# Second attention pass of a quantized transformer block: the side work of the score loop cut into one piece per step, layer-norm groups shifted by two token tiles, the rounding issued behind the evacuations, and the last tiles in pairs

## The chip, the cores and the metric

One NeuronCore of a Trainium2 chip runs the whole program. The metric is the device time of one execution in microseconds (us); lower is better. The engines are TensorE (PE in the profile; its weight loads are PEld), VectorE (DVE), ScalarE (ACT), GpSimd (POOL) and SyncE (SP), which issues DMAs.

## The reference

Four transformer blocks L0 to L3 run one after the other on `x`, 4 sequences of 1024 tokens of 288 features (16 heads of 18). The change lies in block L2 ("Block 2"), a block whose attention is quantized with one scale for a whole tensor:

```python
def _fake_quant(x, n_bits, always_zero=False):
    levels = float(2 ** n_bits - 1)
    if always_zero:
        delta = max(x) / levels;  zp = 0
    else:
        delta = (max(x) - min(x)) / levels;  zp = round(-min(x) / delta)
    xq = clip(round(x / delta) + zp, 0.0, levels)
    return (xq - zp) * delta

def _quant_attention(x, ctx, Wq, Wk, Wv, Wo, bo):
    q, k, v = heads(x @ Wq), heads(ctx @ Wk), heads(ctx @ Wv)
    q, k, v = _fake_quant(q), _fake_quant(k), _fake_quant(v)
    probs = softmax(q k^T / sqrt(HD))
    probs = _fake_quant(probs, always_zero=True)
    return (probs @ v) @ Wo + bo

n1 = _ln(h);  h = h + _quant_attention(n1, n1, Wq1, Wk1, Wv1, Wo1, bo1)
n2 = _ln(h);  h = h + _quant_attention(n2, encoder_hidden_states, Wq2, Wk2, Wv2, Wo2, bo2)
n3 = _ln(h);  ... gated feed-forward ...
```

The self-attention's probabilities are rounded with a scale that needs the largest probability of all heads and rows. So the kernel goes over the scores twice: a first pass finds sums and maxima, the second one computes the scores again, rounds and multiplies by the values. The queries of the cross-attention, `n2 @ Wq2`, need their minimum and maximum over all tokens before they can be rounded.

## The kernel before

The tokens are 32 tiles of 128 (`NT = 32`, 8 to a sequence). `fq_passes` holds both passes. The second pass runs over 8 halves (4 sequences, 2 halves of 512 queries each); each half is one call of `attend_levels`: 4 groups of 4 heads, and in each group 8 steps, one for every 128 keys. So a half has 32 steps and the pass 256. A step does this:

- four matmuls (L3573) put the scores of 4 heads into two PSUM tiles of two banks each; there are three such tiles
- ScalarE takes the exponential of each (L3582, two instructions a step) into `e`, which has two buffers
- VectorE rounds `e` to bfloat16 levels `eb` (L3585; three buffers)
- the values matmuls (L3556) of the step two before are issued from the list `late`; after a group's eighth step VectorE copies the accumulator to `oT` (L3564)
- `aside()` takes one piece of side work from the list `side`, a list of Python generators; a piece ends at a `yield`.

The side work of a half is:

- `shifts`: for 4 tiles of the next half, GpSimd copies three terms into a padded tile (L2556), TensorE transposes it (L2562), and VectorE adds the result to the queries (L2563)
- `output(t0, oT)`: for the 4 tiles of the half before, the output projection (4 float32 matmuls a tile, L3234, each of two TensorE instructions), added to the residual `x` by VectorE (L3244)
- `queries(t0)`: the layer norm of those same 4 tiles, which have to be finished first: statistics (L1437, L1438), a chain of small VectorE instructions for 1/sqrt of the variance (L1442 to L1457), then per tile the norm `h` (VectorE L3256, GpSimd L3260 and L3261), the bias on `x` (GpSimd L1866), three transposes (L3268), their evacuation by VectorE (L3274), the query projection (3 float32 matmuls, L3282), its evacuation (VectorE L3289), a maximum and a minimum (L811, L812), and a store to DRAM (SP, L3291).

The first half has no `output` and no `queries`; those of the last half run after the loop, and then `fq_tail` begins, which needs the minimum and maximum over all of them. Small PSUM tiles (`ps1`) have two buffers, shared by the accumulator of the values, which holds one of them for a group's eight steps, and all side work.

The program is traced in this order, and the framework then orders each engine's instructions itself: an instruction that it takes to be ready may go ahead of an earlier one that it takes not to be. On the chip every engine works through its own list in order, with semaphores for the dependences.

Of the kernel before, what the change touches and what calls it, by code (L numbers as in the profile page):

```python
# [1179 lines left out]
class Fast(Net):  # L1180
# [250 lines left out]
    def norm_stats_slow(self, t0, m, eps):  # L1431
# [4 lines left out]
        for j in range(m):  # L1436
            nc.vector.bn_stats(st[:, j, :], self.x[:, t0 + j, :])  # L1437
            nc.vector.bn_aggr(mv[:, j, :], st[:, j, :])  # L1438
            if j % 4 == 3:
                yield  # L1440
        ve = self.stat([P, NTB], "ve")[:, :m]
# [6 lines left out]
        for k in range(3):  # L1448
            t = self.stat([P, NTB], "lnt")[:, :m]
            nc.vector.scalar_tensor_tensor(t, ve, -0.5, y, ALU.mult, ALU.mult)  # L1450
            nc.vector.tensor_tensor(t, t, y, ALU.mult)
            rstd = self.sm.tile([P, NTB], F32, tag=f"rstd{k}", name="rstd", bufs=8 if k == 2 else 4)
            rstd = rstd[:, :m]
            nc.vector.scalar_tensor_tensor(rstd, t, 1.5, y, ALU.add, ALU.mult)
            y = rstd
        nmr = self.sm.tile([P, NTB], F32, tag="nmr", name="nmr", bufs=8)[:, :m]
# [1536 lines left out]
    def fq_passes(self, w, q, step, raw, rawq, qmx, qmn, side, aside):  # L2993

        tc, nc = self.tc, self.nc
        with ExitStack() as es:
# [230 lines left out]
            def output(t0, oT):  # L3227

                yield
                yield  # L3230
                for j in range(4):
                    ps = self.ps1()
                    for k in range(NG):
                        nc.tensor.matmul(  # L3234
                            ps[:, :C],
                            lhsT=oT[:, k, j * P : (j + 1) * P],
                            rhs=wo[:, k, :],
                            start=(k == 0),
                            stop=(k == NG - 1),
                        )  # L3240
                        if k == 1:
                            yield
                    xt = self.x[:, t0 + j, :]
                    nc.vector.tensor_tensor(xt, xt, ps[:, :C], ALU.add)  # L3244
                    yield

            def queries(t0):

                rstd, nmr, _ = self.norm_stats_of(t0, 4, 1e-5)
                yield  # L3250
                hs, hTs = {}, {}
                for j in range(4 + 3):
                    if j < 4:
                        t = t0 + j
                        h = hs[j] = ot.tile([P, C], F32, tag="h2", name="h2", bufs=3)
                        nc.vector.tensor_scalar(  # L3256
# [5 lines left out]
                        self.add_bias(t, bo2)  # L3262
                        yield

                    if 0 <= j - 2 < 4:
                        ps = self.ps1()
                        for c in range(NC3):
                            nc.tensor.transpose(  # L3268
                                ps[:CK, c * P : (c + 1) * P],
                                hs[j - 2][:, c * CK : (c + 1) * CK],  # L3270
                                self.idf,
                            )
                        hT = hTs[j - 2] = ot.tile([CK, NC3, P], F32, tag="hT2", name="hT2")
                        nc.vector.tensor_copy(  # L3274
                            hT, ps[:CK, : NC3 * P].rearrange("p (c t) -> p c t", t=P)
                        )
                        yield
                    if 0 <= j - 3 < 4:
                        t = t0 + j - 3
                        ps = self.ps1()  # L3280
                        for c in range(NC3):
                            nc.tensor.matmul(  # L3282
                                ps[:, :C], lhsT=hTs[j - 3][:, c, :], rhs=wq2[:, c, :],
                                start=(c == 0), stop=(c == NC3 - 1),
                            )
                            if c == 0:
                                yield
                        y = ot.tile([P, C], F32, tag="y2", name="y2", bufs=1)
                        nc.vector.tensor_copy(y, ps[:, :C])  # L3289
                        self.min_max(qmx[:, t, :], qmn[:, t, :], y.unsqueeze(1))  # L3290
                        nc.sync.dma_start(rawq[t // NTB][:, t % NTB, :], y)  # L3291
                        yield
# [249 lines left out]
    def attend_levels(self, ep, qT, keys, v, b, qh, oT, step, late, aside):  # L3542
# [23 lines left out]
        for g in range(NG):  # L3566
            kz = keys(g)
            for kt in range(NTB):
# [14 lines left out]
                eb = ep.tile([P, 4, 512], BF16, tag="eb", name="eb", bufs=3)  # L3583

                nc.vector.tensor_scalar(eb, e, MAGIC, MAGIC, ALU.add, ALU.subtract)  # L3585
                late.append((values, g, kt, eb))
                if len(late) > 2:
                    st = late.pop(0)
                    st[0](*st[1:])
                aside()  # L3590

# [106 lines left out]
```

## Time and profile before

| | us |
|---|---|
| median of 3 runs | 4913.63 (4906.7 to 4917.26) |
| the profiled execution | 4914.71 |
| its span in the profile | 4913.0 |
| score loop of the second pass (first to last L3582) | 2347.7 to 2900.3 = 552.6 |
| its 8 halves, from the first L3582 of each | 61.1, 71.2, 69.4, 73.4, 69.6, 70.6, 69.5, 67.8 |
| after the loop, to the end of the last L812 | 2900.3 to 2939.1 = 38.8 |

The span is the time from the first to the last instruction of the program in the profile. The halves and their ends are read off the starts of the L3582 instructions in the trace. Busy times of overlapping instructions of one engine are counted once.

### The profile page before, as it was taken

Reading aid. Unit: us, or ns where it says so; the run is one execution under the profiler, and the core shown is the slowest. Engines: PE = TensorE matmul, PEld = TensorE weight load, DVE = VectorE, ACT = ScalarE, POOL = GpSimd, SP = SyncE. Lnnn points to the kernel's source line nnn. Section 1 sums busy time; section 2 is a strip of 40 time slices with the busy share of each in tenths; the row PEclk is TensorE's granted clock in tenths of the full one; section 3 lists DMA queues with packets and bytes.
Section 4 is the critical chain, followed back from the end, with each engine's and each line's share of the span. In section 5 each row is a group of like instructions: output and inputs, shape, how many; then the busy total and the mean of one; then the engine's idle time right before and its main releaser. Section 6 shows DMA issues by size and latency. Waiting matters only on the chain. (4 is left out here: it accounts for less than half of the span.)

```text
span 4913.0 us, 63515 instructions
## 1 busy us (share of the span) xinstructions
PE 4274.3 (87%) x23227; PEld 1733.7 (35%) x23227; DVE 3050.2 (62%) x6797; ACT 2986.3 (61%) x4219; POOL 1164.0 (24%) x1780
## 2 busy tenths in 40 slices
PE   4999998889988979998798873799998999998786
PEld 2223223445565411110233332445453223223444
DVE  8355445876644589999778878334244355445885
ACT  2776775666642279998888854122113776775664
POOL 2001001433212576420112225111111001002553
PEclk9999999889999955555688885799998999998898
DMA  3000002110001221000000022101000000001000
GB/s 85 3 5 22 12 8 72 41 35 16 3 13 56 105 68 33 26 6 0 22 25 25 23 85 57 50 13 34 1 3 15 4 4 22 14 7 40 17 17 18
DMA packets 137699, 135.97 MB, mean 28 GB/s; under 512 B 69276, under 2 KB 114972, under 8 KB 135712
## 3 DMA queue, kind: packets, MB, share of 16 engines
q1 hardware_dynamic: 136176, 128.13, 8.7%
q0 software_dynamic: 1200, 3.69, 0.3%
q8 instruction: 184, 3.01, 0.3%
q14 instruction: 139, 1.14, 0.1%
HBM read 79.92 MB, written 43.47 MB: 25 GB/s over the span
## 5 line engine op out<-in xcount | busy, mean ns | idle before, releaser
L2137 ACT ACTIVATE e<-ps 128x1024 f32<-128x1024 f32 x1024 | 993.7, 1022 | 411.8 <-PE ps L2127 403.9
L2127 PE MATMUL ps<-qT,kT 32*128 32x512 f32 x4096 | 624.6, 648 | 2.3 <-DVE sext L2049 2.3
L3164 DVE TENSOR_REDUCE top<-e 128x2 f32<-128x2048 f32 x256 | 563.6, 2298 | 14.8 <-ACT e L3157 14.6
L2083 PE MATMUL ps<-e,v 128*32 128x512 f32 x4096 | 556.4, 614 | 9.0 <-DVE oT L2094 9.0
L3533 PE MATMUL ps<-qk 32*128 32x512 bf16 x1024 | 499.9, 604 | 40.7 <-ACT e L3157 38.9
L3582 ACT ACTIVATE e<-ps 128x1024 f32<-128x1024 f32 x512 | 484.3, 1055 | 77.6 <-PE ps L3573 60.3
L3157 ACT ACTIVATE e<-ps 128x1024 f32<-128x1024 f32 x512 | 520.6, 1154 | 6.8 <-PE ps L3533 3.7
L1862 POOL TENSOR_TENSOR x<-x,y 128x288 f32<-128x288 f32 x192 | 152.5, 806 | 838.3 <-DVE y L1861 488.5
L3585 DVE TENSOR_SCALAR eb<-e 128x2048 bf16<-128x2048 f32 x256 | 320.5, 1256 | 46.5 <-ACT e L3582 44.1
L3573 PE MATMUL ps<-qk,kz 64*128 64x512 bf16 x1024 | 228.7, 444 | 42.7 <-ACT e L3582 39.3
L2600 PE MATMUL psf<-hT,w 128*128 128x512 f32 x576 | 257.9, 600 | 0.6 <-ACT hT L2592 0.6
L2127 PEld LDWEIGHTS ps<-qT,kT 32*128 32x128 f32 x4096 | 184.9, 185 | 201.3 <-issue 128.2
L2083 PEld LDWEIGHTS ps<-e,v 128*32 128x32 f32 x4096 | 81.3, 108 | 403.5 <-issue 344.3
L3533 PEld LDWEIGHTS <-qk 32*128 32x128 bf16 x1024 | 53.0, 100 | 465.2 <-issue 464.2
L3482 ACT ACTIVATE gl<-psf,bf 128x512 f32<-128x512 f32 x72 | 46.1, 685 | 269.9 <-PE psf L2604 265.5
L1477 POOL TENSOR_TENSOR h<-h,g 128x288 f32<-128x288 f32 x112 | 91.4, 817 | 443.8 <-ACT h L1474 434.2
L3486 DVE SCALAR_TENSOR_TENSOR u<-psf,bf,gl 128x512 f32<-128x512 f32 x72 | 51.2, 747 | 218.2 <-ACT gl L3482 218.2
L1979 POOL TENSOR_TENSOR v<-y,wv1b 128x288 f32<-128x288 f32 x64 | 51.5, 810 | 560.6 <-DVE y L1976 560.6
L278 PEld LDWEIGHTS <-qT 98*128 98x128 bf16 (+2 forms) x1344 | 132.1, 104 | 126.0 <-issue 37.4
L2094 DVE COPY oT<-ps 128x512 f32<-128x512 f32 x64 | 44.2, 690 | 212.1 <-PE ps L2083 212.1
L3157 ACT ACTIVATION_READ_ACCUMULATOR e<-ps 128x1 f32 x512 | 173.3, 338 | 0.0
L2600 PEld LDWEIGHTS psf<-hT,w 128*128 128x128 f32 x576 | 109.7, 192 | 132.9 <-issue 124.0
(526 smaller groups left out, 7825.3 us busy)
## 6 DMA issues: line engine op xcount, KB each, us to landing
raw<-y SPq DMA_DIRECT2D x32, 432.0 KB
in<-raw SPq DMA_DIRECT2D x30, 432.0 KB
kz<-qk SPq DMA_DIRECT2D x128, 64.0 KB
wn<-in_L_wfc SPq DMA_DIRECT2D x12, 432.0 KB
x<-in_x SPq DMA_DIRECT2D x4, 1152.0 KB
vvo<-vt SPq DMA_DIRECT2D x16, 288.0 KB
vo<-vvo SPq DMA_DIRECT2D x4, 1152.0 KB
rawq<-y SPq DMA_DIRECT2D x32, 144.0 KB
```

Source lines behind the costliest of these rows:

```text
L278: self.nc.tensor.matmul(out, lhsT=lhs[:, k, :], rhs=rhs[:, k, c0:c1], start=(k == 0), stop=(k == kc - 1))
L1862: nc.gpsimd.tensor_tensor(self.x[:, t, :], self.x[:, t, :], y, ALU.add)
L2083: nc.tensor.matmul(acc[i * HP : (i + 1) * HP, :], lhsT=st["v"][:, kt, h * (D + 1) : h * (D + 1) + HP], rhs=es_[i // 2][:, i % 2, :], start ...
L2127: nc.tensor.matmul(pss[i // 2][:, i % 2, :], lhsT=self.row_tile(kT, i)[:, kt * P : (kt + 1) * P], rhs=self.row_tile(qT, i)[:, qh * 512 : ( ...
L2137: nc.scalar.activation(e, ps, AF.Exp, scale=SCALE)
L2600: nc.tensor.matmul(o, lhsT=lhs(i)[:, c, :], rhs=rhs(i)[:, c, :], start=(c == 0), stop=False)
L3157: nc.scalar.activation(e[:, j, :].rearrange("p (a n) -> p a n", a=2), sc, AF.Exp, scale=rstep, accum_out=sums[:, t, h0 + j : h0 + j + 1],)
L3164: nc.vector.tensor_reduce(top[:, t, h0 : h0 + 2], e, AX.X, ALU.max)
L3533: self.last = self.nc.tensor.matmul(ps[:, c, :], lhsT=self.row_tile(qT, i)[:, g, qt * P : (qt + 1) * P], rhs=self.row_tile(kT, i)[:, g, c ...
L3573: nc.tensor.matmul(pss[i][:, n, :], lhsT=kz[rows, i, kt * P : (kt + 1) * P], rhs=qT[rows, g, qh * 512 : (qh + 1) * 512], start=True, stop= ...
L3582: nc.scalar.activation(e[:, 2 * n : 2 * n + 2, :], ps, AF.Exp, scale=step)
L3585: nc.vector.tensor_scalar(eb, e, MAGIC, MAGIC, ALU.add, ALU.subtract)
```

## The change

It touches the side work of the second pass, three lines of `attend_levels` and what runs after the loop.

1. One generator per half, `beside_half(n, oT)`, takes the place of `shifts`, `output` and `queries`. A piece is now one of: one tile's shift; one of the 4 matmuls of an output tile (the fourth with the residual add and the tile's statistics); one third of a query tile (transposes and their copy; two matmuls; the third matmul with the copy, maximum, minimum and store). For a middle half this makes 2 + 8 + 8 + 2 + 12 = 32 pieces.
2. The tiles are normalized in groups: {0,1}, {2..5}, ..., {22..25}, {26,27}, {28,29}, {30,31}. A group is complete after the second output tile of a half. Its chain (`norm_chain`, cut into four pieces) and its norms, one tile to a piece, are issued beside the third and fourth output tiles, and its queries follow in the last 12 pieces.
3. In the loop, the norm's scale and shift (L3256 before, on VectorE) is a GpSimd instruction.
4. The tile `hT2` has one buffer where it had two, `h2` has four where it had three.
5. In `attend_levels` the values matmuls of two steps before and the side piece are traced ahead of the rounding of the step.
6. The last half takes group {22..25} and {26,27}; its 36 pieces are 4 more than its steps. After the loop, tiles 28 to 31 go in two pairs: output of two, their norms on VectorE (`norm_dve`), output of two, queries of the first pair, norms of the second, queries of the second. There the evacuations are ScalarE copies.

```diff
--- before.py
+++ after.py
@@ -1438,6 +1438,16 @@
             nc.vector.bn_aggr(mv[:, j, :], st[:, j, :])
             if j % 4 == 3:
                 yield
+        at = self.norm_chain(mv, m, eps)
+        while True:
+            try:
+                next(at)
+            except StopIteration as end:
+                return end.value
+
+    def norm_chain(self, mv, m, eps):
+
+        nc = self.nc
         ve = self.stat([P, NTB], "ve")[:, :m]
         nc.vector.tensor_scalar(ve, mv[:, :, 1], eps, None, ALU.add)
 
@@ -1453,6 +1463,7 @@
             rstd = rstd[:, :m]
             nc.vector.scalar_tensor_tensor(rstd, t, 1.5, y, ALU.add, ALU.mult)
             y = rstd
+            yield
         nmr = self.sm.tile([P, NTB], F32, tag="nmr", name="nmr", bufs=8)[:, :m]
         nc.vector.scalar_tensor_tensor(nmr, mv[:, :, 0], -1.0, rstd, ALU.mult, ALU.mult)
         return rstd, nmr, mv[:, :, 0]
@@ -3224,80 +3235,129 @@
             bo2 = self.load_bc(at, w["bo2"], C, "bo2")
             wq2 = self.load_w(at, w["Wq2"], C, "wq2")
 
-            def output(t0, oT):
-
+            mvs, normed = {}, {}
+            groups = [range(0, 2)] + [range(t, t + 4) for t in range(2, NT - 6, 4)]
+            groups += [range(t, t + 2) for t in range(NT - 6, NT, 2)]
+            group_of = {t: n for n, ts in enumerate(groups) for t in ts}
+
+            def out_tile(t0, oT, j):
+
+                t = t0 + j
+                ps = self.ps1()
+                for k in range(NG):
+                    nc.tensor.matmul(
+                        ps[:, :C],
+                        lhsT=oT[:, k, j * P : (j + 1) * P],
+                        rhs=wo[:, k, :],
+                        start=(k == 0),
+                        stop=(k == NG - 1),
+                    )
+                    if k < NG - 1:
+                        yield
+                xt = self.x[:, t, :]
+                nc.vector.tensor_tensor(xt, xt, ps[:, :C], ALU.add)
+                n = group_of[t]
+                if n not in mvs:
+                    mvs[n] = self.sm.tile([P, NTB, 2], F32, tag="mvk", name="mvk", bufs=8)
+                st = self.sm.tile([P, NTB, 6], F32, tag="st", name="st", bufs=2)
+                nc.vector.bn_stats(st[:, 0, :], xt)
+                nc.vector.bn_aggr(mvs[n][:, t - groups[n][0], :], st[:, 0, :])
                 yield
+
+            def norms(n, dve):
+
+                m = len(groups[n])
+                chain = self.norm_chain(mvs.pop(n)[:, :m], m, 1e-5)
+                while True:
+                    try:
+                        next(chain)
+                    except StopIteration as end:
+                        stats = end.value
+                        break
+                    yield
                 yield
...
+                rstd, nmr, _ = stats
+                for j, t in enumerate(groups[n]):
+                    h = normed[t] = ot.tile([P, C], F32, tag="h2", name="h2", bufs=4)
+                    if dve:
+                        self.norm_dve(h, t, stats, j, g2, b2)
+                    else:
+                        nc.gpsimd.tensor_scalar(
                             h, self.x[:, t, :], rstd[:, j : j + 1], nmr[:, j : j + 1],
                             ALU.mult, ALU.add,
                         )
                         nc.gpsimd.tensor_tensor(h, h, g2, ALU.mult)
                         nc.gpsimd.tensor_tensor(h, h, b2, ALU.add)
-                        self.add_bias(t, bo2)
+                    self.add_bias(t, bo2)
+                    yield
+
+            def query(t, copy):
+
+                h = normed.pop(t)
+                ps = self.ps1()
+                for c in range(NC3):
+                    nc.tensor.transpose(
+                        ps[:CK, c * P : (c + 1) * P], h[:, c * CK : (c + 1) * CK], self.idf
+                    )
+                hT = ot.tile([CK, NC3, P], F32, tag="hT2", name="hT2", bufs=1)
+                copy(hT, ps[:CK, : NC3 * P].rearrange("p (c t) -> p c t", t=P))
+                yield
+                ps = self.ps1()
+                for c in range(NC3):
+                    nc.tensor.matmul(
+                        ps[:, :C], lhsT=hT[:, c, :], rhs=wq2[:, c, :],
+                        start=(c == 0), stop=(c == NC3 - 1),
+                    )
+                    if c == 1:
                         yield
...
+                y = ot.tile([P, C], F32, tag="y2", name="y2", bufs=1)
+                copy(y, ps[:, :C])
+                self.min_max(qmx[:, t, :], qmn[:, t, :], y.unsqueeze(1))
+                nc.sync.dma_start(rawq[t // NTB][:, t % NTB, :], y)
+                yield
+
+            def beside_half(n, oT):
+
+                turns = shifts(*divmod(n + 1, 2)) if n + 1 < 2 * B else iter(())
+                if n:
+                    for _ in range(2):
+                        next(turns, None)
                         yield
...
+                    t0 = 4 * (n - 1)
+                    for j in range(2):
+                        yield from out_tile(t0, oT, j)
+                    extra = norms(n - 1, False)
+                    for j in range(2, 4):
+                        for _ in out_tile(t0, oT, j):
+                            next(extra, None)
+                            yield
+                for _ in turns:
+                    if n:
+                        next(extra, None)
+                    yield
+                if n:
+                    for _ in extra:
+                        pass
+                    extra = norms(n, False) if n == 2 * B - 1 else iter(())
+                    for t in groups[n - 1]:
+                        for _ in query(t, nc.vector.tensor_copy):
+                            next(extra, None)
+                            yield
+                    for _ in extra:
+                        pass
+                    if n == 2 * B - 1:
+                        for t in groups[n]:
+                            yield from query(t, nc.vector.tensor_copy)
 
             late = []
+            oT = None
             for b in range(B):
                 for qh in range(2):
-                    side[:0] = [shifts(*divmod(2 * b + qh + 1, 2))] if 2 * b + qh + 1 < 2 * B else []
+                    n = 2 * b + qh
+                    side.append(beside_half(n, oT))
                     oT = ot.tile([P, NG, 512], F32, tag="oT", name="oT")
 
-                    def keys(g, turn=(2 * b + qh) * NG):
+                    def keys(g, turn=n * NG):
                         if turn + g + 1 < 2 * B * NG:
                             spread(turn + g + 1)
                         return kzs[(turn + g) % 2]
@@ -3305,12 +3365,22 @@
                     self.attend_levels(ep, qk[:, b, 0], keys, v, b, qh, oT, rstep, late, aside)
                     while side:
                         aside()
-                    t0 = b * NTB + qh * 4
-                    side += [output(t0, oT), queries(t0)]
             for st in late:
                 st[0](*st[1:])
-            while side:
-                aside()
+            for n in (2 * B, 2 * B + 1):
+                for t in groups[n]:
+                    for _ in out_tile(NT - 4, oT, t % 4):
+                        pass
+                if n == 2 * B:
+                    for _ in norms(n, True):
+                        pass
+            for n in (2 * B, 2 * B + 1):
+                for t in groups[n]:
+                    for _ in query(t, nc.scalar.copy):
+                        pass
+                if n == 2 * B:
+                    for _ in norms(n + 1, True):
+                        pass
 
     def fq_tail(self, w, kq, keep, rawq, mx, nmn, beside):
 
@@ -3580,14 +3650,13 @@
                 e = ep.tile([P, 4, 512], F32, tag="e", name="e")
                 for n, ps in enumerate(pss):
                     nc.scalar.activation(e[:, 2 * n : 2 * n + 2, :], ps, AF.Exp, scale=step)
-                eb = ep.tile([P, 4, 512], BF16, tag="eb", name="eb", bufs=3)
-
-                nc.vector.tensor_scalar(eb, e, MAGIC, MAGIC, ALU.add, ALU.subtract)
-                late.append((values, g, kt, eb))
-                if len(late) > 2:
+                if len(late) > 1:
                     st = late.pop(0)
                     st[0](*st[1:])
                 aside()
+                eb = ep.tile([P, 4, 512], BF16, tag="eb", name="eb", bufs=3)
+                nc.vector.tensor_scalar(eb, e, MAGIC, MAGIC, ALU.add, ALU.subtract)
+                late.append((values, g, kt, eb))
 
 
 @with_exitstack
```

More of the change, by code (lines that the diff above doesn't have):

```diff
@@ L3225, in fq_passes @@
             wq2 = self.load_w(at, w["Wq2"], C, "wq2")
-            def output(t0, oT):
-                yield
-                yield
[L3231 to L3256, printed above, removed]
+            mvs, normed = {}, {}
+            groups = [range(0, 2)] + [range(t, t + 4) for t in range(2, NT - 6, 4)]
@@ L3261, in queries @@
                         nc.gpsimd.tensor_tensor(h, h, b2, ALU.add)
-                        self.add_bias(t, bo2)
-                        yield
[L3265 to L3276, printed above, removed]
-                        yield
@@ L3278, in queries @@
[L3278 to L3292, printed above, removed]
+                    self.add_bias(t, bo2)
@@ L3582, in attend_levels @@
                     nc.scalar.activation(e[:, 2 * n : 2 * n + 2, :], ps, AF.Exp, scale=step)
+                if len(late) > 1:
+                    st = late.pop(0)
+                    st[0](*st[1:])
+                aside()
                 eb = ep.tile([P, 4, 512], BF16, tag="eb", name="eb", bufs=3)
@@ L3586, in attend_levels @@
                 late.append((values, g, kt, eb))
-                if len(late) > 2:
-                    st = late.pop(0)
-                    st[0](*st[1:])
-                aside()
 @with_exitstack
```

## The prediction, made before the changed kernel was run

> **What bounds the kernel now.** I read the page first, then windows over the second pass, one a half, then the rows of its exponential, and at last the worst stretch inside a half.
>
> ```profile
> 2347.00:2409.00 62.00, 54.10 (x280) 13.06 (x281) 41.73 (x41) 59.50 (x65) 2.48 (x9) 0.60 0.11 27
> ...
> 2623.00:2692.00 69.00, 59.18 (x337) 21.48 (x336) 56.83 (x85) 59.88 (x64) 15.45 (x16) 0.88 0.09 24
> 2692.00:2763.00 71.00, 62.59 (x348) 21.96 (x347) 57.69 (x86) 60.93 (x66) 15.47 (x16) 0.83 0.09 24
> ...
> 2900.00:2939.00 39.00, 24.56 (x70) 16.16 (x65) 18.66 (x47) 0.26 (x1) 11.77 (x17) 0.65 0.46 172
> ```
>
> The columns are PE, PEld, DVE, ACT, POOL busy, the granted TensorE clock, DMA share and GB/s. The first row is half 0, which has only shifts beside it; the next two are middle halves, the last is the stretch after the loop. ScalarE has the same 64 exponentials in each half and is busy near 60 us; half 0 needs 61 us, the middle ones 69 to 71. So each middle half has about 10 us in which ScalarE waits.
>
> ```profile
> L3582 ACT ACTIVATE e<-ps x512: 1016/1032/1218, 2347.7 to 2899.1; 128x1024 f32<-128x1024 f32 x171
> ...
>   PE ps L3573: 60.3, 53
>   DVE eb L3585: 10.9, 25
> ```
>
> ScalarE waits for scores (60.3 us), not for rounding (10.9). Back to back, exponentials start 0.905 us apart in the trace (376 of 511 intervals are under 1 us), so a step costs at least 1.81 us, a half 57.9, eight halves 463. The loop takes 552.6: 89 us of waiting. By steps, half 4 (2622.8 to 2692.4) is at 1.81 to 1.83 through most steps, also where an output matmul, a residual add and statistics ran beside it (10.0 of 10 us ACT busy in 2630 to 2640). It loses 1.4 us in steps 10 to 13, where two output matmuls fall in one step (2.04 a step), and 7.5 us in steps 19 to 22 (2.88, 3.30, 3.31, 5.28):
>
> ```profile
> 2659.00:2676.00 17.00, 13.29 (x53) 4.26 (x51) 11.48 (x15) 10.33 (x11) 13.31 (x12) 0.51 0.03 9
> ...
> ACT e L3582 <- PE ps L3573: 5.3, 4, 2.6
> PEld ps L3268 <- POOL h L3261: 4.5, 2, 3.2
> PE ps L3268 <- POOL h L3261: 3.5, 2, 2.7
> ```
>
> There all four norms start at once, TensorE stands in its queue before a transpose whose `h` GpSimd has not finished, the scores of later steps stand behind it, and the clock is at half when it resumes. Rounding and GpSimd slow one another:
>
> ```profile
> 2660.28 1.81 DVE L3585 TENSOR_SCALAR eb<-e 128x2048 bf16<-128x2048 f32 x1
> ...
> 2660.97 1.77 POOL L3261 TENSOR_TENSOR h<-h,b 128x288 f32<-128x288 f32 x1
> 2662.71 0.79 POOL L3260 TENSOR_TENSOR h<-h,g 128x288 f32<-128x288 f32 x1
> ```
>
> **The change, part by part.**
>
> *Spread and shifted groups.* The pieces fill a middle half: 2 shifts, 8 output matmuls, 8 more beside the norms' chain and norms, 2 shifts, 12 query pieces: 32 for 32 steps. The first transpose of a half comes six steps (10.9 us) after its norm is issued, the next ones every three steps. GpSimd needs for a tile 0.51 (128x288 TENSOR_SCALAR multiply-add, L818) and three times 0.79, 2.9 us against 5.4 us between transposes. The stall of 7.5 us goes; what is late next is TensorE itself. Per step at full clock it needs 0.33 for each of two score pairs and 0.33 for the values (starts in the trace: 2632.14, 2632.47, 2632.79), 0.98; a float32 matmul alone in a step adds 0.66 (two instructions), two in a step 1.17, three transposes 0.47, a shift about 0.3. A query tile then takes 3 x 0.98 + 0.47 + 1.17 + 0.66 = 5.24 of 5.43 us, an output step 1.64 of 1.81. The half: 31.4 + 16 x 0.66 + 4 x 2.3 + 1.2 = 52.4 of 57.9 us. It fits, with 10% to spare, at full clock only: at half clock the same starts are 0.54 apart, the base is 52.2, a float32 matmul 1.08, a query tile 4.1, and the sum 52.2 + 17.3 + 16.3 + 2.2 = 88.
>
> *Clock.* The trace grants 0.5 for 40.96 us of half 0, where TensorE had no side work but no long gap either, and again at 2659.2, after 8 us of plain steps. It returns to 1.0 after one to three windows of 3.41 us in which TensorE is busy throughout (2666.1 to 2676.3 the longest). "TensorE: Matmul & The Clock Gate" of the Trainium skill (section "What's actually happening") lets the clock drop after an idle window of about 3.4 us and rise after a busy one. By that rule no half would be cold and the cost is nothing; by the trace a plain step is too little, and half 1 and half 2 (half 1 has six empty steps at its end) start cold: three windows at 2.7 us a step (1.63 + 1.08) instead of 1.81, 3 us each. I take the trace. In each drop of the loop the window of 3.41 us before it was busy 0.61 or less, and 0.69 or more kept the clock; a plain step is 0.98 of 1.81 = 0.54, a shift step 0.71, an output step 0.91, a query tile 0.96. So from half 3 on the clock should stay.
>
> *VectorE.* It is the tight one: 56.8 us busy in a 69 us half. The norm's four instructions leave (0.43 to 0.90 each, 2 us); all else stays. Rounding starts follow other work after 1.13 us, so a step has 0.68 for side work. By piece: output with add and statistics 1.15; chain 1.2, 0.6, 0.6, 0.2; `hT` 0.53; query end (copy, maximum, minimum) 1.27; `oT` 0.61; shift 0.41. Rounding may be 0.6 us late before `e` (two buffers) holds ScalarE. Carrying the backlog step by step, it passes 0.6 in five steps: where `oT` meets the end of an output tile (1.76; twice), the first chain piece and the last, and where `oT` meets a query end (1.88): 0.48 + 0.52 + 0.51 + 0.48 + 0.6 = 2.6 us a half.
>
> *Evacuations ahead of the rounding.* Rounding of a step can only start when its second exponential ends. In the trace the values matmuls traced in a step, and the side piece after them, run about 2 us before that, so an evacuation is ready before the rounding and hides in VectorE's wait; it frees its PSUM tile up to 1.7 us earlier (1.22 of rounding and 0.45 of copy). But in the trace the residual add of 2645.32 already goes ahead of the rounding at 2645.70, since the framework orders the engine. I give it nothing of its own. If TensorE is late, rounding now waits behind the copy, the values behind that; the two-step lag covers 1.8 us.
>
> *GpSimd.* 16 instead of 12 large instructions a half. "SBUF — State Buffer" of the Trainium skill (section "Who interferes with whom") says that a VectorE instruction in a two-port mode and a GpSimd one shut each other out for the whole instruction. By it one GpSimd instruction fits between two roundings, and 16 steps take 1.22 + 0.80 = 2.02 instead of 1.81: 3.4 us a half. By the rows it is less: rounding averages 1.26 against 1.22 undisturbed over half 4, 1.3 us a half, but at three-microsecond steps. Price bounds 1.3 and 3.4; I take 2. The GpSimd norm is bounded by L818 (0.51) and the L819 form (1.25), 4 x 0.74 = 3 us of GpSimd time that the six steps hide. Spad copies (0.26) queue behind norms, with 14 steps to spare. On SP the stores move to every third step, past the `kz` loads (four a group, a group ahead): nothing, as long as a `y` leaves within 5.4 us.
>
> *Sum of the loop.* Half 0 stays 61.1. A middle half: 57.9 + 2.6 + 2 = 62.5. Half 1: 64; half 2: 65; halves 3 to 6: 250; half 7: 63, four pieces run over. Sum 503, against 552.6: -49.5.
>
> *Tail.* From the last exponential to the last minimum is 38.8 us now; 36.2 of it after the last `oT`. New: four left-over query pieces go ahead on VectorE and put `oT` off by up to 3.5. Then two tiles' output (cold, 8 x 0.48 = 3.9), statistics to 5.1, chain 2.6, two norms of 2 x 0.5 (L1464, L1467) to 8.7; PSUM frees for the transposes after the other pair's adds, 10.9; first query pair to 16.5, its extremes to 17.4; only then the second chain, norms (21.8), two queries with ScalarE copies of 0.6 and one `y` buffer, to 28.2. 6.2 + 28.2 = 34.4: -4.4, between -10 and +3; I take -5.
>
> Against the profiled execution (4914.71, 1.1 above the median): 4914.7 - 54.5 = 4860.2; I say 4860.
>
> **The rivals.**
>
> *VectorE bound:* every GpSimd instruction holds a rounding up by 0.6 (the 1.82 row), 9.6 a half less 3.4 of slack, halves near 66: 61 + 462 = 523, tail 0: 4885. For it: VectorE at 95% of a 57.9 us half. Against: the eight output steps at 1.81.
>
> *The clock stays low* (the slower side): spread thin, side work no longer makes the dense bursts that wake TensorE. With 52.4 us a half at full and 88 at half clock, TensorE alone takes 70.2 us, the mean of halves 1 to 7 now, at a granted clock of 0.69; below that the change loses. At 0.65, near half 0's 0.60, it is 73 us: 61 + 512 = 573, 4914.7 + 20 = 4935. For it: half 0, and the drop after plain steps. Against: a cold TensorE with side work is fully busy, and that woke it each time.
>
> *It does not do what it says:* the framework issues pieces by its own reckoning, the bunches remain, the loop stays at 552, tail -4: 4910, no change.
>
> *Clean:* no lock cost, halves 59.5, tail -8: 4832.
>
> **How the numbers follow.** Main case with the clean end 0.62; VectorE bound 0.20; clock 0.10; no change 0.05; something else slower 0.03. The measurement can tell about 0.2% (10 us). Faster 0.83, same 0.05, slower 0.12. Range 4836 (halves 60, tail -8) to 4896 (past the VectorE case), which leaves out 2 in 10.
>
> **What would show it.** Right: L3582's wait for PE falls from 60 to under 25 us, its wait for rounding rises to some 15 to 25; no step over 3.5 us in halves 3 to 6; PEclk there 0.95 or more; L3268's wait for GpSimd near zero in the loop; the stretch after the loop 30 to 41 us. Wrong: the clock at 0.7 or less in middle halves; L3268 still waiting for GpSimd; roundings mostly at 1.8.

## The result, and the profile after

| | before | after |
|---|---|---|
| median | 4913.24 us (4906.7 to 4917.26, 4 runs) | 4859.46 us (4857.3 to 4862.64, 4 runs) |
| ratio, 95% interval | | 0.9893, 0.9877 to 0.9909 |
| the profiled execution, its span | 4914.71, 4913.0 | 4857.3, 4855.6 |
| up to the first exponential of the loop | 2347.7 | 2337.1 |
| the loop | 552.6 | 502.2 |
| last exponential to last minimum | 38.8 | 36.9 |
| from there to the end | 1973.9 | 1979.4 |

The halves of the loop now take 61.1, 62.8, 64.0, 61.3, 61.2, 61.3, 61.2 and 69.4 us. The change made the kernel faster by 53.8 us in the medians, by 57.4 in the profiled executions: -10.6 before the loop, -50.4 in it, -1.9 after it, +5.5 in the rest. A second set of runs of the same kernel gave 4860.27 (ratio 0.9902, 0.9882 to 0.9921), with the same stretches to 0.2 us.

Here are the windows of the changed kernel that answer to those shown before: half 0, two middle halves (4 and 5), half 7, and the stretch after the loop. The columns are the same: PE, PEld, DVE, ACT, POOL busy, granted clock, DMA share, GB/s.

```profile
2337.00:2398.00 61.00, 53.49 (x280) 12.82 (x276) 41.71 (x40) 59.05 (x64) 1.89 (x8) 0.60 0.10 27
2586.00:2647.00 61.00, 55.35 (x342) 21.05 (x340) 55.02 (x82) 59.38 (x65) 25.06 (x20) 0.97 0.10 28
2647.00:2709.00 62.00, 56.34 (x348) 21.16 (x344) 55.94 (x83) 60.37 (x66) 25.11 (x20) 0.97 0.11 29
2770.00:2839.00 69.00, 60.91 (x328) 22.35 (x329) 58.48 (x93) 60.32 (x65) 26.93 (x24) 0.88 0.07 20
2839.00:2876.00 37.00, 25.33 (x88) 16.54 (x86) 20.55 (x63) 3.69 (x9) 5.49 (x9) 0.79 0.43 143
```

The second and third rows are the result. ScalarE does the same 64 exponentials, busy for 59 to 60 us as before, but now in a half of 61; the 8 to 10 us of waiting are gone, and the granted clock is 0.97 where it was 0.83 to 0.88. GpSimd is busy for 25 us where it was 15. The fourth row is the exception: half 7 has the same ScalarE work and takes 69.4 us.

The exponential's own row (line 3652 now) says what it still waits for; the first number after a releaser is the sum in us, the second how often:

```profile
L3652 ACT ACTIVATE e<-ps x512: 1017/1046/1292, 2337.1 to 2838.3; 128x1024 f32<-128x1024 f32 x171
...
  PE ps L3643: 18.6, 15
  DVE eb L3658: 11.0, 32
```

The wait for scores fell from 60.3 us to 18.6 (9.4 us of either number is one wait, ahead of the loop's first exponential). The wait for rounding stayed where it was. And in the list of waits inside halves 3 to 6 the transposes, for which TensorE had stood in its queue 4.5 and 3.5 us in the one stretch shown before, hardly appear:

```profile
ACT e L3652 <- DVE eb L3658: 5.5, 16, 0.6
...
PEld ps L3299 <- POOL h L3290: 0.9, 2, 0.4
```

These are the sum, the count and the longest: 0.9 us in four halves together.

### The profile page after: what moved, and what is told of

The parts are those of the page before. It is cut to its first block, busy times and chain, and to the rows that moved or that the text cites. A ratio compares the mean times of both kernels' runs of the same rounds, so it can differ in the third digit from the quotient of the medians.

```text
span 4855.6 us, 63549 instructions
## 1 busy us (share of the span) xinstructions
PE 4230.4 (87%) x23227; PEld 1727.3 (36%) x23227; DVE 3038.4 (63%) x6791; ACT 2980.8 (61%) x4227; POOL 1213.9 (25%) x1800
## 5 line engine op out<-in xcount | busy, mean ns | idle before, releaser
L3603 PE MATMUL ps<-qk 32*128 32x512 bf16 x1024 | 499.6, 604 | 40.7 <-ACT e L3168 38.8
L3652 ACT ACTIVATE e<-ps 128x1024 f32<-128x1024 f32 x512 | 477.8, 1078 | 33.8 <-PE ps L3643 18.6
L3658 DVE TENSOR_SCALAR eb<-e 128x2048 bf16<-128x2048 f32 x256 | 324.0, 1271 | 48.2 <-ACT e L3652 47.2
L3643 PE MATMUL ps<-qk,kz 64*128 64x512 bf16 x1024 | 215.9, 419 | 33.2 <-ACT e L3652 28.6
```

The costliest lines, as they stand in the source:

```text
L3603: self.last = self.nc.tensor.matmul(ps[:, c, :], lhsT=self.row_tile(qT, i)[:, g, qt * P : (qt + 1) * P], rhs=self.row_tile(kT, i)[:, g, c ...
L3643: nc.tensor.matmul(pss[i][:, n, :], lhsT=kz[rows, i, kt * P : (kt + 1) * P], rhs=qT[rows, g, qh * 512 : (qh + 1) * 512], start=True, stop= ...
L3652: nc.scalar.activation(e[:, 2 * n : 2 * n + 2, :], ps, AF.Exp, scale=step)
```

## The experiments

Three things above all came at once in the loop: work in smaller pieces, norms that start long before their transposes (their lead), and another order around the rounding. The theory was that the lead of the norms over the transposes carries the gain. The rival was that the fine pieces do (TensorE gets its side work in doses and stays warm), or the order. Times below are read like the table above: the four stretches are those of the profiled execution. Each ratio is to runs of the kernel before taken in the same set (medians 4906.06 to 4909.26 us). The diffs are against the changed kernel except where said.

| kernel | time, us | ratio to before (95%) | before the loop | loop | tail | rest |
|---|---|---|---|---|---|---|
| before, again | 4915.96 | one run | 2344.6 | 560.2 | 37.9 | 1971.5 |
| old order around the rounding | 4859.63 | 0.9894 (0.9875 to 0.9913) | 2342.4 | 502.9 | 36.2 | 1978.2 |
| before with the new order alone | 4895.47 | 0.9978 (0.9971 to 0.9985) | 2345.0 | 552.7 | 39.0 | 1973.8 |
| norm's first instruction on VectorE | 4871.2 | 0.9921 (0.9902 to 0.9940) | 2333.3 | 512.1 | 37.9 | 1985.2 |
| tail in one group of four | 4857.61 | 0.9892 (0.9875 to 0.9909) | 2338.9 | 502.1 | 43.2 | 1971.4 |
| no lead of the norms | 4907.65 | 1.0000 (0.9990 to 1.0009) | 2339.1 | 555.6 | 36.8 | 1972.2 |
| two matmuls to a piece | 4912.9 | 1.0014 (1.0005 to 1.0023) | 2338.1 | 560.7 | 34.3 | 1980.1 |
| bunched matmuls, lead kept | 4861.73 | 0.9914 (0.9895 to 0.9933) | 2336.3 | 496.2 | 36.6 | 1982.5 |
| half of the norm's GpSimd work | 4853.55 | 0.9887 (0.9871 to 0.9904) | 2337.1 | 494.5 | 37.7 | 1982.1 |
| less VectorE work in a query | 4839.85 | one run | 2344.0 | 488.8 | 33.4 | 1971.9 |
| four at the end, on ScalarE | 4851.29 | 0.9886 (0.9869 to 0.9903) | 2344.5 | 500.5 | 35.8 | 1971.7 |

### No lead of the norms

```diff
-            groups = [range(0, 2)] + [range(t, t + 4) for t in range(2, NT - 6, 4)]
-            groups += [range(t, t + 2) for t in range(NT - 6, NT, 2)]
+            groups = [range(t, t + 4) for t in range(0, NT, 4)]
...
-                    for j in range(2):
+                    for j in range(4):
                         yield from out_tile(t0, oT, j)
                     extra = norms(n - 1, False)
-                    for j in range(2, 4):
-                        for _ in out_tile(t0, oT, j):
-                            next(extra, None)
-                            yield
...
```

After the loop the last four tiles go as one group. Pieces are still one to a step, but what two shift pieces leave of the chain and the norms is issued at once, right ahead of the first query piece. The buffers of `h2` and `hT2` are those of the changed kernel.

> The changed kernel with the norm groups not shifted: a group is the four tiles of one half, so its norms can only be issued right before its queries; the pieces stay one a step, and the last four tiles run as before the change. Theory (the lead of six steps is what takes the stall away): TensorE waits for GpSimd before the first transposes of each half again, steps of 3 to 5 us, halves 66 to 70, 4890 to 4915. Rival (spreading alone carries the gain): halves 61 to 63, 4855 to 4870.

The whole gain of the loop was gone: 555.6 us. Halves 4 to 6 take 68.3 us each, with one step of 8.2 us at the same place; halves 1 and 7 take 75.4. The list of waits around that step of half 4:

```profile
ACT e L3638 <- PE ps L3629: 6.1, 2, 3.2
PEld ps L3298 <- POOL h L3289: 4.0, 1, 4.0
DVE hT L3302 <- PE ps L3298: 3.7, 1, 3.7
PE ps L3298 <- POOL h L3289: 3.7, 1, 3.7
```

This is the stall of the kernel before again: the transposes wait for the norm of GpSimd, and the exponential waits for scores that stand behind them. Spreading without the lead only moves it.

### Bunched matmuls, with and without the lead

In the first of two kernels an output tile is two pieces of two matmuls each:

```diff
-                    if k < NG - 1:
+                    if k == 1:
                         yield
```

> The changed kernel with two output matmuls in a piece in place of one: 24 pieces a middle half, eight empty steps at its end, norms and queries earlier by up to eight steps relative to the half's end. Theory (TensorE holds 1.81 a step only with one float32 matmul, and plain steps let its clock drop): output steps of about 2.05 and a cold start of every half, halves 64 to 67, 4875 to 4900. Rival (only the lead of the norms matters): halves 61 to 62.5, 4855 to 4865.

This missed what I expected of it: 560.7 us, middle halves of 69 to 71. But the edit also halved the pieces beside which the norms are issued, so that the first transposes follow their norm after two steps in place of six: half 4 has steps of 4.55 and 3.73 us there. It changed two things, so the grain was tried a second time with an empty piece after each pair of matmuls, which keeps the lead:

```diff
-                    if k < NG - 1:
+                    if k == 1:
                         yield
+                        yield
...
                 nc.vector.bn_aggr(mvs[n][:, t - groups[n][0], :], st[:, 0, :])
                 yield
+                yield
```

> The changed kernel with two output matmuls in one piece and an empty piece after it: the same 32 pieces, the same lead of the norms, only the matmuls bunched. In the run with two matmuls a piece the lead was cut too, so that run could not tell the two apart. Theory (the lead is what counts; two steps of TensorE work, 3.3 us, still fit in 3.6): halves 3 to 6 at 61 to 62, total within 8 us of the changed kernel. Rival (the grain counts by itself): output steps of 2.04 us, halves 63 or more, 12 us or more slower.

Now halves 3 to 6 take 61.2 us each, as in the changed kernel; the loop of the profiled execution is even 6.0 us shorter, all of it in halves 1, 2 and 7, though the median of the runs is not (4861.73 against 4859.46). The window of half 4:

```profile
2583.00:2644.00 61.00, 55.02 (x340) 21.53 (x336) 55.14 (x81) 59.28 (x65) 25.06 (x20) 0.97 0.10 28
```

It is the row of the changed kernel, clock included. So one matmul to a step is not what makes the gain, and neither is it what keeps the clock up. The kernels part by the lead: with it the stall is gone at either grain, with the lead cut the stall is there at either grain.

### The order around the rounding

One kernel undoes it in the changed kernel, the other does it alone in the kernel before. The first:

```diff
-                if len(late) > 1:
-                    st = late.pop(0)
-                    st[0](*st[1:])
-                aside()
                 eb = ep.tile([P, 4, 512], BF16, tag="eb", name="eb", bufs=3)
                 nc.vector.tensor_scalar(eb, e, MAGIC, MAGIC, ALU.add, ALU.subtract)
                 late.append((values, g, kt, eb))
+                if len(late) > 2:
+                    st = late.pop(0)
+                    st[0](*st[1:])
+                aside()
```

> The changed kernel with the rounding of a step traced first again, then the values of two steps before and the side piece. Theory (the framework orders VectorE itself, the traced order is worth nothing): within 10 us of the changed kernel, 4850 to 4870. Rival (the evacuations ahead of the rounding carry part of the gain): halves 3 to 6 go from 61.2 to 64 or more, 4880 or more.

> The kernel before with one part of the change alone: the values of two steps before and the side piece traced ahead of the rounding. Theory (worth nothing by itself, the stall on the norms stays): ratio to before 0.998 to 1.001. Rival (it frees PSUM earlier and so carries part of the gain): 0.996 or less.

In the changed kernel the order is worth nothing in sum (loop 502.9 against 502.2, medians 4859.63 against 4859.46), though halves 1 to 3 are 0.4 to 1.8 us longer and half 7 is 3.2 shorter. Alone it gave 0.9978, 0.15 to 0.29% less than before: about 11 us in the medians (4895.47 against 4906.06), a fifth of the whole gain, and a little more than I had expected. The two changes do not add up, then. Where these 11 us lie was not found: the profiled execution (4912.18) is the slowest of its 20, and its loop is 552.7, that of before. The loop of before is itself not steady: a second profile of the kernel, run as a yardstick, had 560.2.

> The kernel before once more, for a second profile. Every instruction ahead of the loop is issued in the same order in before and in the changed kernel, and yet the loop starts at 2347.7 us in the one profile of before and at 2337.1 and 2337.0 in two of the changed kernel. Theory (it belongs to the program, not to the run): 2347 to 2349 again. Rival (chance of a run): anywhere from 2333 to 2348, as in the other kernels.

### The norm's first instruction back on VectorE

```diff
-                        nc.gpsimd.tensor_scalar(
+                        nc.vector.tensor_scalar(
```

> The changed kernel with the norm's scale and shift back on VectorE in the loop. Theory (VectorE is nearly full, its backlog is what is left of waiting): 2 to 3.6 us more VectorE work a half, of which 1 to 2 show: 4866 to 4874, and L3652 waits longer for the rounding. Rival (the lock between GpSimd and VectorE is the larger cost): one GpSimd instruction a tile fewer, 4845 to 4858.

The loop grew by 9.9 us, halves 3 to 6 by 1.3 to 2.2 each, above all in step 15 (2.82 us for 1.81), and the exponential's wait for rounding from 11.0 to 15.1 us. VectorE has no room left for 2 us a half, so this move to GpSimd is a real, small part of the gain.

### What is left in a middle half: GpSimd and VectorE

A middle half is 3.3 us above 32 undisturbed steps (57.9). The prediction put 2 us on GpSimd and 2.6 on VectorE. One kernel drops two lines, 8 of the 16 large GpSimd instructions of a half:

```diff
-                        nc.gpsimd.tensor_tensor(h, h, g2, ALU.mult)
-                        nc.gpsimd.tensor_tensor(h, h, b2, ALU.add)
```

> The changed kernel without the multiplication by the norm's gain and the addition of its shift in the loop (left out of the computation): 8 large GpSimd instructions a half instead of 16. Theory (GpSimd and rounding lock each other out; priced at 2 us a half in the prediction, 3.3 us of waiting are left a half): halves 3 to 6 at 59 to 60, 8 to 15 us faster than the changed kernel, mean rounding nearer 1.22. Rival (what is left is VectorE's own backlog): halves within 0.5 us of 61.2.

Halves 3, 5 and 6 became shorter by 0.4 to 0.8 us; half 4 became 0.6 longer, with 6.8 us at half clock (2618.0 to 2624.8) where the changed kernel has 3.4. On average over the four that is 0.35 us; half of the 2 us that I had priced would be 1. The rows of the rounding, of the changed kernel and of this one (minimum, median, maximum in ns):

```profile
L3658 DVE TENSOR_SCALAR eb<-e x256: 1189/1226/1868, 2339.9 to 2839.3; 128x2048 bf16<-128x2048 f32 x128
```

```profile
L3656 DVE TENSOR_SCALAR eb<-e x256: 1192/1224/1491, 2339.9 to 2831.6; 128x2048 bf16<-128x2048 f32 x128
```

The median does not move, but the mean goes from 1271 to 1230 ns. In halves 3 to 6 it goes from 1283 to 1229, with 36 roundings over 1.30 us in the changed kernel and 5 in this one. VectorE thus pays 1.7 us a half for meeting these 8, of which the exponential sees little: its wait for rounding falls from 11.0 to 6.9 us in the whole loop. The larger stretch is on the other side. GpSimd's groups in halves 3 to 6 of the changed kernel (busy us, mean ns):

```profile
L1877 POOL TENSOR_TENSOR x<-x,bo 128x288 f32<-128x288 f32 x16 | 28.4, 1777 | 0.0
L3289 POOL TENSOR_TENSOR h<-h,g 128x288 f32<-128x288 f32 x16 | 24.4, 1527 | 0.0
L3285 POOL TENSOR_SCALAR h<-x,rstd,nmr 128x288 f32<-128x288 f32 x16 | 20.9, 1313 | 91.2 <-DVE nmr L1468 91.2
L3290 POOL TENSOR_TENSOR h<-h,b 128x288 f32<-128x288 f32 x16 | 20.5, 1284 | 0.0
```

Instructions of this shape with two tensors (L1877, L3289, L3290) take 0.79 us at their shortest and 1.28 to 1.78 on average beside the roundings. It is GpSimd that stretches most, and GpSimd has the time: it is busy for 25 us of 61.

The other shortens VectorE's maximum and minimum at the end of a query:

```diff
-                self.min_max(qmx[:, t, :], qmn[:, t, :], y.unsqueeze(1))
+                self.min_max(qmx[:, t, :], qmn[:, t, :], y[:, :32].unsqueeze(1))
```

> The changed kernel with the maximum and the minimum of each query tile taken over 32 of its 288 columns (the rest is left out of the computation): about 0.5 us less VectorE work a query tile, 2 us of a half's 55. Theory (the waiting left in halves 3 to 6, 3.3 us each, is VectorE's backlog, half of it where a query tile ends): these halves at 59.5 to 60.3. Rival (it is TensorE's or the lock's): within 0.3 us of 61.2.

```profile
2588.00:2648.00 60.00, 55.31 (x345) 20.56 (x342) 53.73 (x84) 59.40 (x66) 26.47 (x20) 0.97 0.11 29
```

Halves 3 to 6 took 59.7 to 59.8 us, 1.5 less, with the same clock. So a little under half of the 3.3 us is VectorE being late where a query tile ends. This is one run, and the other 1.8 us were not isolated.

### The tail, and half 7

```diff
-            groups += [range(t, t + 2) for t in range(NT - 6, NT, 2)]
+            groups += [range(NT - 6, NT - 4), range(NT - 4, NT)]
...
+            for t in groups[2 * B]:
+                for _ in out_tile(NT - 4, oT, t % 4):
+                    pass
+            for _ in norms(2 * B, False):
+                pass
+            for t in groups[2 * B]:
+                for _ in query(t, nc.vector.tensor_copy):
+                    pass
```

> The changed kernel with the last four tiles in one group after the loop: all four outputs, one chain, norms on GpSimd, queries evacuated by VectorE. Theory (the pairs save what the first profiles differ by, 36.9 against 38.8, plus the left-over pieces that go ahead): the stretch after the loop 39 to 44 us, 3 to 7 us slower than the changed kernel. Rival (pairs save nothing, their second chain costs what they win): within 2 us.

The tail became 6.3 us longer, and the total stayed the same, since the rest became 8.0 us shorter. The pairs win their time and it is given back in the next stage, the first pass of the cross-attention. The loss can be placed: counted from the last minimum, the two kernels' TensorE instructions, which come in the same order, are 0.1 us apart at first, and 8.9 apart at the 188th (82.1 us against 73.2; about 4 at the 200th, 7 at the 300th). The waits of that stretch, for the changed kernel and then for this one:

```profile
PEld L3432 <- DVE pads L3426: 24.2, 12, 4.2
```

```profile
PEld L3426 <- DVE pads L3420: 19.7, 10, 4.5
```

The sum, the count and the longest again: TensorE waits 4.5 us longer for VectorE's `pads`, which is about half of the loss. All engines but VectorE issue this stage in the same order in all kernels. VectorE has one order, from the 41st instruction after the last minimum, in the six kernels with this tail in pairs and a rest of 1978.2 to 1985.2 us; it has the order of before in five with a rest of 1971.4 to 1973.9; and the kernel with smaller extremes, in pairs too, leaves the order of before for 21 places only and has 1971.9. So the ordering that the framework chose goes with the loss in every kernel, but no run forced the order alone.

The last kernel tried to keep both, with the four tiles in one group, their norms on VectorE and copies on ScalarE, and to relieve half 7 of its two empty pieces:

```diff
-            groups += [range(t, t + 2) for t in range(NT - 6, NT, 2)]
+            groups += [range(NT - 6, NT - 4), range(NT - 4, NT)]
...
-                    for _ in range(2):
+                    for _ in range(2 if n < 2 * B - 1 else 0):
...
+            for _ in norms(2 * B, True):
+                pass
+            for t in groups[2 * B]:
+                for _ in query(t, nc.scalar.copy):
+                    pass
```

> The changed kernel with the last four tiles in one group (norms on VectorE, ScalarE copies) and the last half without its two empty pieces. In all kernels with pairs at the end the framework issues VectorE's instructions of the stage after it in another order, and everything after the last minimum takes 1978 to 1985 us where it takes 1971 to 1974 in the others. Theory (the order costs 6 us or so, which is what the pairs win): the order of before returns, the rest is 1971 to 1974, the stretch after the loop 38 to 42, the last half 64 to 68: 4848 to 4856, faster than the changed kernel. Rival (the rest depends on something else): rest 1978 or more, 4859 to 4866.

The tail is 35.8 us and the rest 1971.7: pairs were not needed. Half 7 stayed at 70.2, a miss. The time is 4851.29, with a ratio to before of 0.9886 (0.9869 to 0.9903). That is the shortest of the kernels that compute everything, but the interval overlaps that of the changed kernel, so I call it no more than that; loop, tail and rest together are 10.5 us shorter in the two profiles.

A repeat of the changed kernel asked whether half 7 is chance:

> The changed kernel once more, for a second profile of the same program. Theory: the loop takes 500 to 503 us again, halves 3 to 6 about 61.2; half 7 (69.4 us in the first profile) lost its 8 us to a drop of the TensorE clock[...], so it may come out anywhere from 62 to 70. Rival: half 7 is slow by its own instruction order and repeats 69 within 1 us. The start of the loop, 10.5 us earlier than in the profile of before, comes from stages that the change does not touch; if that is chance, it moves by several us here.

It is not: 69.4 again, step for step within 0.1 us. Of its 11.5 us over the floor, 9.1 lie in two places. Steps 10 to 14 (2.84, 2.78, 2.21, 2.49, 2.03: 3.3 us over) come right behind two steps (8 and 9) in which TensorE has no side work, and fall in a stretch whose clock is 0.72 (2786 to 2798). Steps 20 to 24 (3.68, 2.56, 1.82, 4.43, 2.33: 5.8 us over) hold the chain and the norms of the second group beside queries. The windows over both, and then the timelines of VectorE and GpSimd in the second (start, duration):

```profile
2786.00:2798.00 12.00, 10.81 (x48) 3.29 (x47) 8.72 (x23) 9.93 (x11) 2.80 (x5) 0.72 0.00 1
2805.00:2821.00 16.00, 12.25 (x64) 4.77 (x63) 15.29 (x29) 12.44 (x13) 10.11 (x10) 0.85 0.03 9
```

```profile
2810.53 0.76 DVE L1456 TENSOR_SCALAR lny<-ve 128x2 int32<-128x2 int32 x1
2811.32 0.72 DVE L1457 TENSOR_SCALAR lny<-lny 128x2 int32<-128x2 int32 x1
2812.08 0.71 DVE L1460 SCALAR_TENSOR_TENSOR lnt<-ve,lny 128x2 f32<-128x2 f32 x1
```

```profile
2809.42 1.84 POOL L3290 TENSOR_TENSOR h<-h,b 128x288 f32<-128x288 f32 x1
2811.22 0.80 POOL L3289 TENSOR_TENSOR h<-h,g 128x288 f32<-128x288 f32 x1
2811.97 0.79 POOL L1877 TENSOR_TENSOR x<-x,bo 128x288 f32<-128x288 f32 x1
2812.72 0.79 POOL L3290 TENSOR_TENSOR h<-h,b 128x288 f32<-128x288 f32 x1
```

VectorE is full (15.29 of 16 us), and the small instructions of the chain, on two columns, each end within 0.03 us of the end of a GpSimd instruction (2811.29 beside 2811.26, 2812.04 beside 2812.02). The row of that line over the whole program has a minimum of 133 ns:

```profile
L1456 DVE TENSOR_SCALAR lny<-ve x50: 133/170/800, 16.6 to 4798.0; 128x4 int32<-128x4 int32 x30, 128x8 int32<-128x8 int32 x16, 128x2 int32<-128x2 int32 x4
```

With half of the norm's GpSimd instructions, steps 20 to 24 are 1.0 us over instead of 5.8, and half 7 takes 64.1; with bunched matmuls steps 10 to 14 are 0.4 over, but steps 19 to 24 still 5.2. So the second place comes from GpSimd's instructions; the half clock from 2816.2 to 2826.4, behind the stall, is part of its 5.8 us. For the first, the slow clock stands in the profile. Halves 4 and 5 have a drop as well, also behind two steps without TensorE side work, but it lasts 3.4 us instead of 6.8 and falls on two shift steps and the first transposes, steps of 1.81 to 1.92. Why half 7's is longer was not isolated.

## Why the prediction was right, and where it was not

**The stall and its cause.** Right, and the kernel without the lead shows it: take the lead away and the gain of the loop is gone, with fine pieces, the new order and the changed buffers still there. The score wait fell to 18.6 us (under 25 was expected); no step of halves 3 to 6 is over 2.5 us (3.5); their clock is 0.97 to 1.00 (0.95); the transposes' wait for GpSimd is 0.9 us. The two places named in half 4 of before held 8.9 of its 11.7 us over 57.9; the largest of the others, step 30 with 3.00 us, is gone too (1.82).

**Sum of the loop.** 503 predicted, 502.2 measured, but by offsetting terms, so the close hit is in part luck. Halves 3 to 6 were put at 62.5 and took 61.2 or 61.3; halves 1 and 2 at 64 and 65, and took 62.8 and 64.0; half 7 at 63, and took 69.4.

**GpSimd's 2 us a half.** Mis-sized: half of its instructions are worth 0.35 us. The roundings do stretch, by 1.7 us a half, near the lower of my two prices (1.3), but most of that does not reach the exponential, and GpSimd stretches more. The higher price, 3.4, was my reading of "SBUF — State Buffer" in the Trainium skill (section "Who interferes with whom"), by which, between GpSimd and a VectorE instruction in a two-port mode, whoever issues first keeps the shared ports for the whole instruction and the other waits. I had let the rounding wait each time. The trace agrees with the rule in the chain of half 7, where VectorE's instructions end with GpSimd's; in halves 3 to 6 it was mostly GpSimd that took longer.

**VectorE's 2.6 us a half.** Shown only in part: of the 3.3 us, 1.5 go with a smaller query end, where the sum had 0.6, and the rest was not isolated. The mark that went with it failed: the wait for rounding was to rise to 15 to 25 us and stayed at 11.0.

**Half 7.** The term that failed. I gave it half a microsecond for "four pieces run over" (63 for 62.5) and priced neither its second group of norms with their chain beside queries (5.8 us) nor a cold stretch (3.3).

**The clock.** The idea that plain steps let it drop and that dense side work keeps it was right for halves 1 and 2, which start cold (steps of 2.2 to 2.8 us), and nearly so for halves 3 to 6: in halves 4 and 5 the clock still drops for 3.41 us. The two figures, 0.61 for a drop and 0.69 for none, mark no edge: in the changed kernel windows of 3.41 us with TensorE busy for 0.64, 0.66 and 0.67 were followed by a drop, one with 0.65 was not. Of the rivals, the slow one (a clock under 0.69) did not come: the lowest clock of halves 1 to 7 is 0.88. Nor did the one in which every GpSimd instruction holds a rounding up (halves near 66).

**The order around the rounding.** Costed at nothing; in the changed kernel it is nothing, in the kernel before some 11 us.

**The tail.** -5 predicted, -1.9 measured, inside its bounds. What I did not price is the next stage, +5.5, which goes with another order of VectorE's instructions there.

**Outside the loop.** "Nothing" was wrong by -10.6 before the loop. Every engine has the same instructions in the same order there in both kernels, yet the programs of this study start the loop between 2333.3 and 2347.7 us; of the two that were profiled twice, after repeats itself to 0.1 us and before to 3.1. The cause stays open. With the +5.5 it makes -5.1; loop and tail alone are -52.3, which would be 4862.4 for the profiled execution. So 4860 stands closer to the measured 4859.46 than its terms deserve: the loop came as summed, the tail gave 3.1 us less, and -5.1 came from where nothing was expected.

## What to carry to other kernels

When a short engine feeds a transpose or a matmul in the queue that also feeds the bounding engine, give its result a lead of a few steps; how finely the other work was cut mattered much less here. Check the end of a schedule separately, where two groups fall into one turn. And measure the total, not the stage: the time won in the tail here was lost again in the next stage, together with a change of one engine's issue order there.

## What I had not expected of the hardware

- GpSimd's 128x288 instructions with two tensors took 0.79 us at their shortest and 1.28 to 1.78 on average beside the roundings, while the mean rounding of halves 3 to 6 rose only from 1.23 (with half of the norm's GpSimd work) to 1.28.
- VectorE instructions on two columns took 0.71 to 0.76 us beside GpSimd, where the first of these lines has a minimum of 0.13.
- GpSimd's norm, one instruction with multiply and add on 128x288, took 0.57 us at its shortest in this kernel, as the similar line of the prediction (0.51), not the 1.25 of the other form.
